# Transformer block on one core: values in seven block products in place of eight, spread over four slots

## The chip, the cores and the metric

The kernel runs on one core of a Trainium2 chip. The core has a matrix engine (PE, with its weight loads shown apart as PEld), a vector engine (DVE), a scalar engine (ACT), a general one (POOL) and a queue that only issues transfers here (SP). The metric is device time in microseconds, the median of several runs; a profile of one further execution tells where the time goes.

## What is computed

A batch of 16 sequences of 512 tokens and width 256 goes through a layer norm, and then through attention (8 heads of width 128) and a three-layer network side by side; both are added to the input. All of it is in float32.

```python
xn = _layernorm(x, axis=-1)
q = rope(einsum('bim,mhd->bhid', xn, wq))
k = rope(einsum('bim,mhd->bhid', xn, wk))
v = einsum('bim,mhd->bhid', xn, wv)
s = einsum('bhid,bhjd->bhij', q, k) / 128
p = softmax(s - 1e30 * (i < j))
o = einsum('bhij,bhjd->bhid', p, v)
attn = einsum('bhid,hdm->bim', o, wo)
h = s0 * (concat([xn, -xn]) @ where(k0, 1., -1.))   # 512 -> 1024
h = s1 * (2 * relu(h) @ where(k1, 1., -1.))         # 1024 -> 1024
h = s2 * (2 * relu(h) @ where(k2, 1., -1.))         # 1024 -> 256
out = x + attn + h
```

The part that is changed is `v`: for each sequence a product of 512 tokens by 256 inputs with weights of 256 inputs by 1024 outputs (8 heads of 128).

## The kernel before

**Slots.** The work is cut into 128 slots, one for each sequence `b` and head `h` (`g = 8 b + h`), and two more to finish. In slot `g` the core computes the four rows of scores of head `g` (`score_row`, L448), the queries and keys of head `g + 1` (`project_qk`), the turned softmax of head `g` (`turn`, L467, by way of DRAM: `bounce_p` out, `pT` back), the output projection of head `g - 2` (`project_o`, L511), the product of probabilities and values of head `g - 1` (`attend`, L485), and pieces of the network: one tile of layer 1 (`ffn1`, L559, 16 passes with two for each of 8 blocks) and of layer 2 (`ffn2`, L511); layer 0 (`ffn0`, L544) is all in the slot of head 0.

**Order.** The order of instructions on PE, SP and POOL is the order of the program text, written out by hand with generators: `some(gen, n)` runs `n` steps of one, `rest(gen)` what is left. On DVE and ACT a planner with a cost model chooses the order (apart from the first microseconds on DVE); `behind(instruction, after)` only keeps an instruction after another one of the same engine. Every engine then works through its list strictly in order, and waits on semaphores that are set for it.

**Queries and keys in seven products.** `project_qk` uses Strassen's scheme: the 2 x 2 blocks of the tokens (two input halves by two token halves) and of the weights (wq and wk of one head, two input halves each) need seven products of 256 columns where eight would be direct. Combined weights stand in `w7_sb` (made once by `make_w7`, L614 and its scalings at L610 and L612), combined tokens in `tts[b]` (`make_ts`, L348, in the slot of head 6 for the next sequence). The products (L409) go to two PSUM tiles, `pa` and `pb`; ACT copies `ca` (L417), `cb` (L421) and `cu` (L425) out on the way, and DVE adds up: q in L429 and L430, k in L435. Then `rotate` copies halves (ACT, L373 and L374), multiplies (DVE, L376; POOL, L379) and adds (POOL, L381). In a slot the steps lie so: four products at its start; row 0 of the scores; the product S2; layer 2 of the network (8 passes); the product S4 and the sums and rotation of q; row 1; four passes of layer 1; the product WK0 and the sum of k; row 2; and so on.

**Values.** `project_v` is direct. For each sequence and half `gv` of the heads (512 columns) it makes four token tiles, each of two matmuls of 512 columns into one PSUM tile `pv` (L362), copied by ACT into `vt` (L366). The half `gv = 0` of the next sequence is done whole at the end of the slot of head 7, the half `gv = 1` at the end of the slot of head 2:

```python
        if h == 2:
            for gv in range(1, HD // (VH * D)):
                rest(project_v(b, gv))
        if h == H - 1 and b + 1 < B:
            rest(project_v(b + 1, 0))
```

**Buffers.** `pa`, `pb`, `pv` and the tiles `ph` of the network (L544, L559) share a PSUM pool of three buffers that are handed out in turn. A tile `ph` is freed by its two readers, `h1h` (ACT, L567) and `h1l` (DVE, L568). `ca`, `cb` and `cu` have one buffer each, the turned softmax `z` has two.

Of the kernel before, what the change touches and what calls it, by code (L numbers as in the profile page):

```python
# [9 lines left out]
F32 = mybir.dt.float32  # L10
# [3 lines left out]
ALU = mybir.AluOpType  # L14
# [8 lines left out]
def kernel(  # L23
# [81 lines left out]
        (nc.scalar if c % 2 else nc.sync).dma_start(x_first[:, c, :], x[0, ts(c, P), :])  # L105

    xs, x_sums = {}, {}
    wv_sb = wpool.tile([P, NM, HD], F32, tag="wv", name="wv_sb")

    w7_sb = wpool.tile([P, 7, HD], F32, tag="w7", name="w7_sb")  # L110
    WQ0, WQ1, WK0, S1, S2, WK1, S4 = range(7)

    def load_w(engine, sb, w, h0, h1):
        engine.dma_start(
# [20 lines left out]
    def load_k1(f):  # L135
        k1s[f] = wpool.tile([P, NF0, P], U8, tag="k1", name=f"k1_{f}", bufs=2)
        nc.sync.dma_start(k1s[f], k1.rearrange("(c p) f -> p c f", p=P)[:, :, ts(f, P)])

    def load_w1(b, f):

        if (b, f) == (1, 0):
            nc.sync.dma_start(w1_dram[NF1 - 1], w1s[0, NF1 - 1].bitcast(F32))
        if 0 < b < B:
            w1s[b, f] = wpool.tile([P, NF0, P], F32R, tag="w1", name=f"w1_{b}_{f}", bufs=2)
            nc.sync.dma_start(w1s[b, f].bitcast(F32), w1_dram[f])
        elif b == 0:
            if f:
                nc.sync.dma_start(w1_dram[f - 1], w1s[0, f - 1].bitcast(F32))
            if f + 1 < NF1:
                load_k1(f + 1)  # L150
# [4 lines left out]
    nc.scalar.dma_start(sin_sb, sin_t)  # L155
    for i, s in enumerate((s0, s1, s2)):
        nc.scalar.dma_start(s_sb[:, i : i + 1], s.partition_broadcast(P))
    load_w(nc.sync, wv_sb, wv, 0, VH)
    for c in range(NM):
        nc.sync.dma_start(k0_sb[:, c], k0.rearrange("(i c p) f -> c p i f", p=P, c=NM)[c])  # L160
    for h0, h1 in ((2, 4), (4, H)):
        load_w(nc.sync, w7_sb[:, WQ0 : WQ1 + 1], wq, h0, h1)
        load_wk(nc.sync, h0, h1)
    load_k1(0)
    load_w(nc.sync, wv_sb, wv, VH, H)
    xs[1] = load_x(1, "x")
    nc.sync.dma_start(wo_sb, wo.rearrange("h d m -> d h m"))
    nc.sync.dma_start(k2_sb, k2.rearrange("(c p) f -> p c f", p=P))
# [184 lines left out]
    def block(ic, jc):  # L353
        return ic * (ic + 1) // 2 + jc

    def project_v(b, g):
        vt = work.tile([P, NT, VH * D], F32, tag="v", name=f"v_{b}_{g}")
        vts[b, g] = vt
        for c in range(NT):
            pv = ps_mm.tile([P, T], F32, tag="mm", name=f"pv_{b}_{g}_{c}")  # L360
            for m in range(NM):
                nc.tensor.matmul(  # L362
                    pv, tokens(xnTs[b], m)[:, c], wv_sb[:, m, ts(g, VH * D)],
                    start=(m == 0), stop=(m == NM - 1),
                )
            nc.scalar.copy(vt[:, c, :], pv)  # L366
            yield

    def rotate(src, name, g, engine):

# [19 lines left out]
                )  # L390
            rest(rotate(pq, name, g, engine))

    def project_qk(g):

        b, h = divmod(g, H)
        n = half_tokens
        pa = ps_mm.tile([P, T], F32, tag="mm", name=f"pa_{g}")
        pb = ps_mm.tile([P, T], F32, tag="mm", name=f"pb_{g}")

        def product(out_, place, right, **marks):
            nc.tensor.matmul(  # L409
                out_, w7_sb[:, place, ts(h, D)], right, skip_group_check=True, **marks  # L410
            )

        t = tts[b]
        product(pa[:, :n], WQ0, xn_half(b, 0, 0), start=True, stop=False)
        product(pa[:, n:], WQ1, xn_half(b, 1, 0), start=False, stop=True)
        ca = work.tile([P, T], F32, tag="ca", name=f"ca_{g}", bufs=1)
        nc.scalar.copy(ca, pa)  # L417
        product(pb[:, n:], S1, t[:, 0], start=True, stop=False)
        product(pb[:, :n], WK1, t[:, 3], start=False, stop=True)
        cb = work.tile([P, T], F32, tag="cb", name=f"cb_{g}", bufs=1)  # L420
        nc.scalar.copy(cb, pb)  # L421
        yield
        product(pa[:, :n], S2, t[:, 1], start=False, stop=False)
        cu = work.tile([P, n], F32, tag="cu", name=f"cu_{g}", bufs=1)
        nc.scalar.copy(cu, pa[:, :n])  # L425
        yield
        product(pb[:, n:], S4, xn_half(b, 1, 1), start=False, stop=True)
        q = work.tile([P, T], F32, tag="qk", name=f"q_{g}")
        nc.vector.tensor_tensor(q[:, :n], ca[:, :n], ca[:, n:], ALU.add)  # L429
        nc.vector.tensor_tensor(q[:, n:], cu, pb[:, n:], ALU.add)  # L430
        rest(rotate(q, "q", g, nc.gpsimd))
        yield
        product(pa[:, :n], WK0, t[:, 2], start=False, stop=True)
        k = work.tile([P, T], F32, tag="qk", name=f"k_{g}")
        nc.vector.tensor_tensor(  # L435
            k.rearrange("p (i t) -> p i t", i=2),
            pa[:, :n].unsqueeze(1).broadcast_to([P, 2, n]),
            cb.rearrange("p (i t) -> p i t", i=2), ALU.add,
        )
        yield from rotate(k, "k", g, nc.gpsimd)  # L440
        yield

    def score_row(g, ic):
# [18 lines left out]

    def turn(g, after):

        zs = work.tile([P, NQ, NB, Q], F32, tag="z", name=f"z_{g}")
        for ic, p in enumerate(probs.pop(g)):
            behind(nc.vector.transpose(  # L467
                zs[:, :, block(ic, 0) : block(ic + 1, 0), :].rearrange("p j c a -> p c j a"),
                p.rearrange("p (c j a) -> p c j a", j=NQ, a=Q),
            ), after)  # L470
        bounce = carry_out(zs.rearrange("p j n a -> p j (n a)"), "bounce_p", g)
        pT = work.tile([P, NQ, NB, Q], F32, tag="pT", name=f"pT_{g}")
        carry_back(pT.rearrange("p i n a -> p i (n a)"), bounce)
        pTs[g] = pT
# [124 lines left out]
                else:  # L599
                    behind(engine.tensor_scalar(cols, cols, scale, None, ALU.mult), after)  # L600

    def make_w7(h0, h1, reduced, raised, scaled):


        w = [w7_sb[:, i, h0 * D : h1 * D] for i in range(7)]
        for place, scale in (
            (WK1, -K_SCALE), (WK0, K_SCALE), (WQ0, Q_SCALE), (WQ1, Q_SCALE)
        ):
            if not scaled:
                behind(nc.scalar.mul(w[place], w[place], scale), raised)  # L610
            elif place == WK1:
                behind(nc.scalar.mul(w[place], w[place], -1.0), raised)  # L612
        for out_, a, c in ((S1, WK0, WK1), (S2, S1, WQ0), (S4, WQ1, S2), (WK0, WQ0, WK0)):
            behind(nc.vector.tensor_tensor(w[out_], w[a], w[c], ALU.subtract), reduced)  # L614

    def first_slot():
        l0 = [ffn0(0, f) for f in range(NF0)]
        rest(project_v(0, 0))
        project_qk_directly(1, nc.gpsimd)
        for ic in range(NT):  # L620
            reduced, raised = score_row(0, ic)
            rest(l0[ic])
        make_w7(2, 4, reduced, raised, False)
        turn(0, reduced)
        rest(*l0[NT:])
        make_w1(0, reduced, raised)
        load_w1(0, 0)
        for i in range(4):
            make_ts(0, i, reduced)

    def slot_of_head_0(g):

# [17 lines left out]
        for ic in range(NT):  # L650
            reduced, _ = score_row(g, ic)
            if ic == 0:
                some(qk, 1)
                rest(ffn2(b - 1, NF1 - 2))
                some(qk, 1)
            elif ic == 1:
                some(tile, NF0)
                some(qk, 1)
                rest(tile)
            elif ic == 2:  # L660
                some(qk, 1)
                rest(l0[0])
            else:
                rest(qk)
                rest(l0[1])
        turn(g, reduced)
        project_o(g - 2)
        rest(l0[2], l0[3])
# [21 lines left out]
    def slot_of_head_1(g):  # L690
        b = g // H
        qk = tile = iter(())
        if b < B:
            load_w1(b, 1)
            qk = project_qk(g + 1)
            tile = ffn1(b, 0)
        some(qk, 1)
        for ic, n in enumerate((0, 4, 3, 3)):
            if b < B:
                reduced, raised = score_row(g, ic)  # L700
                between_rows(b, 1, ic, reduced, raised)
            if ic == 0:
                some(qk, 1)
                if g > 1:
                    project_o(g - 2)
                some(qk, 1)
            some(tile, n)
            if ic:
                some(qk, 1)
        rest(qk)  # L710
        if g == 1:
            make_w2(reduced)
            make_w7(4, H, reduced, raised, False)
        if b == 0:
            make_w1(1, reduced, raised)
        if b < B:
# [8 lines left out]
    def slot(g):  # L725
# [8 lines left out]
                carry_xn_back(b + 1)  # L734
        qk = project_qk(g + 1) if g + 1 < N_SLOTS else iter(())
        tile = ffn1(b, h - 1)
        some(qk, 1)
        for ic in range(NT):
            reduced, raised = score_row(g, ic)
            between_rows(b, h, ic, reduced, raised)  # L740
            if ic == 0:
                some(qk, 1)
                rest(ffn2(b, h - 2))
                some(qk, 1)
            else:
                some(tile, 4)
                some(qk, 1)
        rest(qk)
        turn(g, reduced)
        project_o(g - 2)  # L750
        rest(tile)
        attend(g - 1)
        if b == 0:
            make_w1(h, reduced, raised)
        if g == 2:
            make_w7(0, 2, reduced, raised, True)
        if h == 2:
            for gv in range(1, HD // (VH * D)):
                rest(project_v(b, gv))
        if h == H - 1 and b + 1 < B:  # L760
            rest(project_v(b + 1, 0))

    E = mybir.EngineType
    with tc.manual_schedule(engines={E.PE, E.SP, E.Pool}):
# [63 lines left out]
```

## Time and profile before

Three runs took 2134.32 to 2135.04 us, with a median of 2134.46 us.

| what | value |
|---|---|
| profiled execution | 2136.97 us |
| its span | 2135.2 us |
| mean granted clock of PE | 0.998 |
| values, PE passes (L362) | 512 records of 128x512, 16 together take 6.87 us |
| queries and keys, PE passes (L409) | 504 + 504 on pa, 504 + 252 on pb, 128x256 |
| sums on DVE, mean | L429 426 ns, L430 421 ns |
| copies on ACT, mean | L366 586 ns, L417 586 ns, L425 352 ns |
| DVE busy, five stretches of 133 us | some 83 us each |

In the lists of groups, each line has the program line, the engine, the operation, output and inputs by name, the shape and the count; then busy time and mean duration of one, and then the idle time of the engine just ahead of them. The granted clock is at 90% or more in all forty slices of the span. The slot of an ordinary head takes 13.78 us of PE, that of head 0 some 22 us, and the ones of heads 2 and 7 have the 6.87 us of values on top.

### The profile page before, as it was taken

The page shows a single profiled execution, that of the slowest core. Times are in us where ns is not written, and L with a number is a line of the kernel's source. Part 1 is how long each engine was busy: PE and PEld are TensorE (multiplying, and loading weights), DVE is VectorE, ACT ScalarE, POOL GpSimd, SP SyncE. Part 2 cuts the span into 40 slices and gives each one's busy share as a digit, 9 for nine tenths or more (in the row PEclk, how much of TensorE's full clock was granted, in tenths as well). Part 3 has the DMA queues.
Part 4 walks back from the last instruction along what each step waited for, and adds up shares of the span by engine and source line. Part 5 has one row for each costly group of instructions (what it writes and reads, how often), then busy time and mean ns, then how long its engine had stood idle before and what let it go on. Part 6 is the DMA issues. An engine that isn't in the chain of part 4 may idle for free.

```text
span 2135.2 us, 31368 instructions
## 1 busy us (share of the span) xinstructions
PE 2116.1 (99%) x10492; PEld 1695.4 (79%) x10492; DVE 1331.9 (62%) x3479; ACT 1082.8 (51%) x2348; POOL 1007.4 (47%) x1064
## 2 busy tenths in 40 slices
PE   8999999999999999999999999999999999999998
PEld 4777878778777787877878778887787877878787
DVE  7666665666656666566665666656656666566654
ACT  5454554554554555455554555555545555555543
POOL 3544544545445454544544445444554535445343
PEclk9999999999999999999999999999999999999999
DMA  5454435445354453544445444453453534544344
GB/s 165 143 161 124 136 102 160 132 124 148 102 164 115 124 159 106 152 126 124 147 123 148 126 123 147 121 155 115 134 146 114 146 114 136 156 121 127 104 140 122
DMA packets 163041, 284.40 MB, mean 133 GB/s; under 512 B 26560, under 2 KB 126912, under 8 KB 162880
## 3 DMA queue, kind: packets, MB, share of 16 engines
q1 hardware_dynamic: 161744, 281.61, 45.2%
q8 instruction: 83, 1.36, 0.3%
q10 hardware_dynamic: 1136, 0.79, 0.1%
q14 instruction: 78, 0.64, 0.1%
HBM read 178.00 MB, written 104.33 MB: 132 GB/s over the span
## 4 chain that ended last, share of the span: by engine, by line
PE 97%; DVE 0%; issue 0%; ACT 0%
PE ph L559 22%; PE y L511 16%; PE po L485 13%; PE s L448 13%; PE pa L409 10%; PE pv L362 10%; PE pb L409 8%; PE ph L544 5%; DVE w_sb L614 0%; DVE z L467 0%; DVE oT L491 0%; DVE x_sum L529 0%; ACT h1h L567 0%; DVE h1l L568 0%
## 5 line engine op out<-in xcount | busy, mean ns | idle before, releaser
L459 POOL TENSOR_SCALAR p<-p,rl 128x128 f32<-128x128 f32 (+3 forms) x512 | 308.3, 606 | 788.3 <-DVE rl L458 787.3
L559 PE MATMUL ph<-h0h,w 128*128 128x512 f32 x1024 | 520.9, 509 | 0.0
L559 PE MATMUL ph<-h0l,w 128*128 128x512 f32 x1024 | 409.6, 400 | 0.0
L448 PE MATMUL s<-kT,qT 128*128 128x128 f32 (+3 forms) x1024 | 359.8, 433 | 0.9 <-POOL kT L381 0.9
L467 DVE STREAM_TRANSPOSE z<-p 128x128 f32<-128x128 f32 (+3 forms) x512 | 245.9, 497 | 146.5 <-POOL p L459 142.2
L456 ACT ACTIVATE p<-p,least 128x128 f32<-128x128 f32 (+3 forms) x512 | 287.6, 562 | 63.7 <-DVE least L451 56.6
L485 PEld LDWEIGHTS po<-pT,v 128*128 128x128 f32 x2560 | 305.4, 192 | 11.2
L379 POOL TENSOR_TENSOR swq<-swq,sin_sb 128x512 f32<-128x512 f32 x127 | 166.2, 1309 | 300.2 <-ACT swq L374 294.5
L485 PE MATMUL po<-pT,v 128*128 128x128 f32 x2560 | 306.2, 275 | 0.0
L451 DVE CUSTOM_DVE_ANT_0 p<-s,causal 128x128 f32<-128x128 f32 (+3 forms) x512 | 248.2, 485 | 27.3 <-PE s L448 25.3
L559 PEld LDWEIGHTS ph<-h0l,w 128*128 128x128 f32 x1024 | 193.8, 189 | 72.4 <-issue 26.9
L559 PEld LDWEIGHTS ph<-h0h,w 128*128 128x128 f32 x1024 | 193.6, 189 | 72.3 <-issue 26.9
L511 PE MATMUL y<-wo_sb,oT 128*128 128x256 f32 x1024 | 241.9, 379 | 0.8 <-DVE oT L491 0.8
L429 DVE TENSOR_TENSOR q<-ca 128x256 f32<-128x256 f32 x126 | 53.6, 426 | 286.4 <-ACT ca L417 286.4
L362 PE MATMUL pv<-wv_sb,xnT 128*128 128x512 f32 x512 | 225.3, 592 | 0.0
L448 PEld LDWEIGHTS s<-kT,qT 128*128 128x128 f32 x1024 | 193.7, 189 | 33.8 <-POOL kT L381 1.3
L511 PEld LDWEIGHTS y<-wo_sb,oT 128*128 128x128 f32 x1024 | 194.0, 190 | 31.5 <-DVE oT L491 1.0
L381 POOL TENSOR_TENSOR qT<-qT,swq 128x512 f32<-128x512 f32 x127 | 196.2, 1545 | 10.0
L366 ACT COPY v<-pv 128x512 f32<-128x512 f32 x128 | 75.0, 586 | 209.9 <-PE pv L362 209.7
L417 ACT COPY ca<-pa 128x512 f32<-128x512 f32 x126 | 73.8, 586 | 210.6 <-PE pa L409 210.6
L362 PEld LDWEIGHTS pv<-wv_sb,xnT 128*128 128x128 f32 x512 | 94.8, 190 | 107.9 <-issue 106.4
L379 POOL TENSOR_TENSOR swk<-swk,sin_sb 128x512 f32<-128x512 f32 x127 | 164.2, 1293 | 0.0
(95 smaller groups left out, 3309.3 us busy)
## 6 DMA issues: line engine op xcount, KB each, us to landing
bounce_p<-z SPq DMA_DIRECT2D x128, 640.0 KB, 2.9
pT<-bounce_p SPq DMA_DIRECT2D x512, 160.0 KB, 3.3
w<-w_dram SPq DMA_DIRECT2D x120, 512.0 KB, 4.8
x_sum<-in_L_attn_x_dram SPq DMA_DIRECT2D x64, 128.0 KB, 5.5
out_dram<-x_sum SPq DMA_DIRECT2D x64, 128.0 KB, 3.3
x<-in_L_attn_x_dram SPq DMA_DIRECT2D x60, 128.0 KB, 5.9
bounce_x<-zx SPq DMA_DIRECT2D x15, 512.0 KB, 6.2
xnT<-bounce_x SPq DMA_DIRECT2D x60, 128.0 KB, 5.8
```

Source lines behind the costliest of these rows:

```text
L362: nc.tensor.matmul(pv, tokens(xnTs[b], m)[:, c], wv_sb[:, m, ts(g, VH * D)], start=(m == 0), stop=(m == NM - 1),)
L379: engine.tensor_tensor(sw, sw, sin_sb, ALU.mult)
L381: engine.tensor_tensor(rt, rt, sw, ALU.add)
L409: nc.tensor.matmul(out_, w7_sb[:, place, ts(h, D)], right, skip_group_check=True, **marks)
L448: nc.tensor.matmul(ps[:, :n], qT[:, ts(ic, P)], kT[:, :n], start=True, stop=True)
L451: reduced = nc.vector.tensor_tensor_reduce(out=p, in0=ps[:, :n], in1=causal[:, T - n :], scale=1.0, scalar=3e38, op0=ALU.add, op1=ALU.min, ...
L456: raised = nc.scalar.activation(p, p, AF.Exp, bias=least, scale=-1.0, accum_out=l)
L459: nc.gpsimd.tensor_scalar(p, p, rl, 1.0, ALU.mult, ALU.mult)
L467: behind(nc.vector.transpose(zs[:, :, block(ic, 0) : block(ic + 1, 0), :].rearrange("p j c a -> p c j a"), p.rearrange("p (c j a) -> p c j ...
L485: nc.tensor.matmul(po[:, ts(ic, P)], vt[:, jc, ts(h % VH, D)], pT[:, :, block(ic, jc), :], start=(jc == 0 and ic == 0), stop=(jc == ic), s ...
L511: nc.tensor.matmul(ys[b][c // 2][:, c % 2, :], lhsT[:, ts(c, P)], rhs, start=(y_done[b][c] == 0 and c % 2 == 0), stop=(y_done[b][c] == N_Y ...
L559: nc.tensor.matmul(ph, w1s[b, f][:, c], h0s[b][i][:, c, :], start=(c == 0 and i == 0), stop=(c == NF0 - 1 and i == 1),)
```

## The change

The values use the same seven products as queries and keys. The blocks are two input halves by two token tiles (`t` and `t + 2`), and two input halves by two column halves of 256 (`VN`, two heads each). Stationary operand is a tile of 128 tokens, combined or plain, moving are 256 columns of combined weights. One piece is `project_v(b, gv, t)` for `t` 0 or 1, so there are four for each sequence: (0, 0) in the slot of head 7 of the sequence before, (0, 1) in the slot of head 1, (1, 0) and (1, 1) in the slots of heads 2 and 3. Only the half `gv = 0` of the first sequence stays direct (`project_v_directly`), since its combined weights and tokens aren't there yet. The seven-product code is taken out of `project_qk` into a generator that both use; with it the last two products, S4 and A21 (`WK0` before), come one right behind the other, and q and k are summed together. `wv_sb` becomes `wv7_sb` with seven places, loaded in two transfers for each half in place of one, and combined by `make_w7_v`, for `gv = 1` at the end of the first slot and for `gv = 0` in slot 2. The tile `z` has one buffer in place of two.

```diff
-    wv_sb = wpool.tile([P, NM, HD], F32, tag="wv", name="wv_sb")
-    WQ0, WQ1, WK0, S1, S2, WK1, S4 = range(7)
+    A11, A12, A21, S1, S2, A22, S4 = range(7)
+    WQ0, WQ1, WK0, WK1 = A11, A12, A21, A22
+    NG = HD // (VH * D)
+    VN = VH * D // 2
+    wv7_sb = wpool.tile([P, 7, NG, VN], F32, tag="wv7", name="wv7_sb")
...
+    def load_wv(gv):
+        for c, places in enumerate(((A11, A21), (A12, A22))):
+            nc.sync.dma_start(
+                wv7_sb[:, places[0] : places[1] + 1 : places[1] - places[0], gv],
+                wv[ts(c, P), gv * VH : (gv + 1) * VH, :].rearrange(
+                    "p (i h) d -> p i (h d)", i=2
+                ),
+            )
...
+    def project_v_directly(b, gv):
+        new_v(b, gv)
         for c in range(NT):
-            pv = ps_mm.tile([P, T], F32, tag="mm", name=f"pv_{b}_{g}_{c}")
-            for m in range(NM):
-                nc.tensor.matmul(
-                    pv, tokens(xnTs[b], m)[:, c], wv_sb[:, m, ts(g, VH * D)],
-                    start=(m == 0), stop=(m == NM - 1),
-                )
-            nc.scalar.copy(vt[:, c, :], pv)
-            yield
+            pv = ps_mm.tile([P, T], F32, tag="mm", name=f"pv_{b}_{gv}_{c}")
+            for i, places in enumerate(((A11, A12), (A21, A22))):
+                for m in range(NM):
+                    nc.tensor.matmul(
+                        pv[:, ts(i, VN)], tokens(xnTs[b], m)[:, c], wv7_sb[:, places[m], gv],
+                        start=(i == 0 and m == 0), stop=(m == NM - 1), skip_group_check=True,
+                    )
+            nc.scalar.copy(vts[b, gv][:, c, :], pv)
...
+    def seven_products(name, b, product):
+        n = half_tokens
+        pa = ps_mm.tile([P, T], F32, tag="mm", name=f"pa_{name}")
+        pb = ps_mm.tile([P, T], F32, tag="mm", name=f"pb_{name}")
+        t = tts[b]
+        product(pa[:, :n], A11, xn_half(b, 0, 0), start=True, stop=False)
+        product(pa[:, n:], A12, xn_half(b, 1, 0), start=False, stop=True)
+        ca = work.tile([P, T], F32, tag="ca", name=f"ca_{name}", bufs=1)
+        nc.scalar.copy(ca, pa)
+        product(pb[:, n:], S1, t[:, 0], start=True, stop=False)
+        product(pb[:, :n], A22, t[:, 3], start=False, stop=True)
+        cb = work.tile([P, T], F32, tag="cb", name=f"cb_{name}", bufs=1)
+        nc.scalar.copy(cb, pb)
+        yield
+        product(pa[:, :n], S2, t[:, 1], start=False, stop=False)
+        cu = work.tile([P, n], F32, tag="cu", name=f"cu_{name}", bufs=1)
+        nc.scalar.copy(cu, pa[:, :n])
+        yield
+        product(pb[:, n:], S4, xn_half(b, 1, 1), start=False, stop=True)
+        product(pa[:, :n], A21, t[:, 2], start=False, stop=True)
+        yield (
+            (ca[:, :n], ca[:, n:]), (cu, pb[:, n:]),
+            (pa[:, :n].unsqueeze(1).broadcast_to([P, 2, n]),
+             cb.rearrange("p (i t) -> p i t", i=2)),
+        )
...
     def project_qk(g):
...
+        for sums in seven_products(f"qk_{g}", b, product):
+            if sums is None:
+                yield
+        q = work.tile([P, T], F32, tag="qk", name=f"q_{g}")
+        k = work.tile([P, T], F32, tag="qk", name=f"k_{g}")
+        nc.vector.tensor_tensor(q[:, :n], *sums[0], ALU.add)
+        nc.vector.tensor_tensor(q[:, n:], *sums[1], ALU.add)
+        rest(rotate(q, "q", g, nc.gpsimd))
+        nc.vector.tensor_tensor(k.rearrange("p (i t) -> p i t", i=2), *sums[2], ALU.add)
+        yield from rotate(k, "k", g, nc.gpsimd)
         yield
+
+    def project_v(b, gv, t):
+        if t == 0:
+            new_v(b, gv)
+        vt = vts[b, gv]
+
+        def product(out_, place, right, **marks):
+            nc.tensor.matmul(
+                out_, right[:, t], wv7_sb[:, place, gv], skip_group_check=True, **marks
+            )
+
+        for sums in seven_products(f"v_{b}_{gv}_{t}", b, product):
+            if sums is None:
+                yield
+        nc.vector.tensor_tensor(vt[:, t, :VN], *sums[0], ALU.add)
+        nc.vector.tensor_tensor(vt[:, t + 2, :VN], *sums[1], ALU.add)
+        nc.vector.tensor_tensor(vt[:, t : t + 3 : 2, VN:], *sums[2], ALU.add)
+        yield
...
-        zs = work.tile([P, NQ, NB, Q], F32, tag="z", name=f"z_{g}")
+        zs = work.tile([P, NQ, NB, Q], F32, tag="z", name=f"z_{g}", bufs=1)
...
+    def make_w7_v(gv, *after):
+        make_w7([wv7_sb[:, i, gv] for i in range(7)], 1.0, 1.0, *after)
...
     def slot_of_head_1(g):
...
+        v = project_v(b, 0, 1) if 0 < b < B else iter(())
         some(qk, 1)
         for ic, n in enumerate((0, 4, 3, 3)):
...
             some(tile, n)
-            if ic:
+            if ic == 2:
+                some(v, 1)
+            if ic > 1:
                 some(qk, 1)
         rest(qk)
+        some(v, 1)
+        some(tile, 3)
+        rest(v)
...
     def slot(g):
...
+        v = iter(())
+        if h in (2, 3):
+            v = project_v(b, 1, h - 2)
+        elif h == H - 1 and b + 1 < B:
+            v = project_v(b + 1, 0, 0)
...
             else:
                 some(tile, 4)
-                some(qk, 1)
+                if ic > 1:
+                    some(qk, 1)
+            if ic == 2:
+                some(v, 1)
         rest(qk)
         turn(g, reduced)
+        some(v, 1)
         project_o(g - 2)
+        rest(v)
         rest(tile)
         attend(g - 1)
...
-        if h == 2:
-            for gv in range(1, HD // (VH * D)):
-                rest(project_v(b, gv))
-        if h == H - 1 and b + 1 < B:
-            rest(project_v(b + 1, 0))
```

The slot of head 0 is shortened by one step of queries and keys in the same way. In the slot of head 1 the piece's sums stand ahead of `turn` and of the last three passes of layer 1, which are followed by `attend`.

More of the change, by code (lines that the diff above doesn't have):

```diff
@@ L157 @@
         nc.scalar.dma_start(s_sb[:, i : i + 1], s.partition_broadcast(P))
-    load_w(nc.sync, wv_sb, wv, 0, VH)
+    load_wv(0)
     for c in range(NM):
@@ L164 @@
     load_k1(0)
-    load_w(nc.sync, wv_sb, wv, VH, H)
+    for gv in range(1, NG):
+        load_wv(gv)
     xs[1] = load_x(1, "x")
@@ L354, in block, with new_v @@
         return ic * (ic + 1) // 2 + jc
-    def project_v(b, g):
-        vt = work.tile([P, NT, VH * D], F32, tag="v", name=f"v_{b}_{g}")
-        vts[b, g] = vt
+    def new_v(b, gv):
+        vts[b, gv] = work.tile([P, NT, VH * D], F32, tag="v", name=f"v_{b}_{gv}")
+    def project_v_directly(b, gv):
+        new_v(b, gv)
         for c in range(NT):
-            pv = ps_mm.tile([P, T], F32, tag="mm", name=f"pv_{b}_{g}_{c}")
-            for m in range(NM):
-                nc.tensor.matmul(
-                    pv, tokens(xnTs[b], m)[:, c], wv_sb[:, m, ts(g, VH * D)],
-                    start=(m == 0), stop=(m == NM - 1),
-                )
-            nc.scalar.copy(vt[:, c, :], pv)
-            yield
+            pv = ps_mm.tile([P, T], F32, tag="mm", name=f"pv_{b}_{gv}_{c}")
[6 more added lines that the diff above has]
+            nc.scalar.copy(vts[b, gv][:, c, :], pv)
     def rotate(src, name, g, engine):
@@ L404, in project_qk @@
         n = half_tokens
-        pa = ps_mm.tile([P, T], F32, tag="mm", name=f"pa_{g}")
-        pb = ps_mm.tile([P, T], F32, tag="mm", name=f"pb_{g}")
         def product(out_, place, right, **marks):
@@ L411, in product @@
             )
[L413 to L421, printed above, removed]
@@ L422, in project_qk @@
-        yield
[L423 to L440, printed above, removed]
+        for sums in seven_products(f"qk_{g}", b, product):
+            if sums is None:
+                yield
@@ L600, in scale_first, with make_w7, make_w7_qk @@
                     behind(engine.tensor_scalar(cols, cols, scale, None, ALU.mult), after)
-    def make_w7(h0, h1, reduced, raised, scaled):
-        w = [w7_sb[:, i, h0 * D : h1 * D] for i in range(7)]
[L606 to L614, printed above, removed]
+    def make_w7(w, scale1, scale2, reduced, raised):
+        for place, scale in ((A22, -scale2), (A21, scale2), (A11, scale1), (A12, scale1)):
+            if scale != 1.0:
+                behind(nc.scalar.mul(w[place], w[place], scale), raised)
+        for out_, a, c in (
+            (S1, A21, A22), (S2, S1, A11), (S4, A12, S2), (A21, A11, A21)
+        ):
+            behind(nc.vector.tensor_tensor(w[out_], w[a], w[c], ALU.subtract), reduced)
+    def make_w7_qk(h0, h1, scaled, *after):
+        w = [w7_sb[:, i, h0 * D : h1 * D] for i in range(7)]
+        make_w7(w, *((1.0, 1.0) if scaled else (Q_SCALE, K_SCALE)), *after)
+    def make_w7_v(gv, *after):
+        make_w7([wv7_sb[:, i, gv] for i in range(7)], 1.0, 1.0, *after)
     def first_slot():
         l0 = [ffn0(0, f) for f in range(NF0)]
-        rest(project_v(0, 0))
+        project_v_directly(0, 0)
         project_qk_directly(1, nc.gpsimd)
@@ L622, in first_slot @@
             rest(l0[ic])
-        make_w7(2, 4, reduced, raised, False)
+        make_w7_qk(2, 4, False, reduced, raised)
         turn(0, reduced)
@@ L629, in first_slot @@
             make_ts(0, i, reduced)
+        for gv in range(1, NG):
+            make_w7_v(gv, reduced, raised)
     def slot_of_head_0(g):
@@ L656, in slot_of_head_0 @@
             elif ic == 1:
-                some(tile, NF0)
+                rest(tile)
+            else:
                 some(qk, 1)
-                rest(tile)
-            elif ic == 2:
-                some(qk, 1)
[L662 to L665, printed above, removed]
+                rest(l0[ic - 2])
+        rest(qk)
         turn(g, reduced)
@@ L707, in slot_of_head_1 @@
             some(tile, n)
-            if ic:
+            if ic == 2:
+                some(v, 1)
+            if ic > 1:
                 some(qk, 1)
         rest(qk)
+        some(v, 1)
+        some(tile, 3)
+        rest(v)
         if g == 1:
             make_w2(reduced)
-            make_w7(4, H, reduced, raised, False)
+            make_w7_qk(4, H, False, reduced, raised)
         if b == 0:
@@ L746, in slot @@
                 some(tile, 4)
-                some(qk, 1)
+                if ic > 1:
+                    some(qk, 1)
+            if ic == 2:
+                some(v, 1)
         rest(qk)
         turn(g, reduced)
+        some(v, 1)
         project_o(g - 2)
+        rest(v)
         rest(tile)
@@ L755, in slot @@
         if g == 2:
-            make_w7(0, 2, reduced, raised, True)
-        if h == 2:
-            for gv in range(1, HD // (VH * D)):
-                rest(project_v(b, gv))
-        if h == H - 1 and b + 1 < B:
-            rest(project_v(b + 1, 0))
+            make_w7_qk(0, 2, True, reduced, raised)
+            make_w7_v(0, reduced, raised)
     E = mybir.EngineType
```

## The prediction

> **What bounds it now.** I read the page's shares first, then the waits of TensorE, then its chain in order of time over one batch, and last what the other engines did in the same slot.
>
> ```profile
> PE 2116.1 (99%) x10492; PEld 1695.4 (79%) x10492; DVE 1331.9 (62%) x3479; ACT 1082.8 (51%) x2348; POOL 1007.4 (47%) x1064
> PE 97%; DVE 0%; issue 0%; ACT 0%
> L362 PE MATMUL pv<-wv_sb,xnT 128*128 128x512 f32 x512 | 225.3, 592 | 0.0
> ```
> A busy PE alone proves little, since ends of matmuls are modelled. The waits decide it:
>
> ```profile
> PE pxn L316 <- DVE xn L257: 8.1, 1, 8.1
> PE ph L544 <- DVE h0l L552: 1.6, 2, 1.3
> PE y L511 <- DVE h1l L568: 1.4, 1, 1.4
> PE s L448 <- POOL kT L381: 0.9, 1, 0.9
> ```
> All seven PE waits sum to 13.6 us: 12.6 in the first 58 us, 1.0 in the tail. Between, PE never waits, so the time is the number of passes through the array, as long as the other engines stay ahead. The chain of waits around slot 7 of one batch (start us, length us, passes) gives the price of a pass:
>
> ```profile
> 527.12 0.86 PE pa L409 x4
> 527.98 0.86 PE pb L409 x4
> 528.84 0.22 PE s L448 x2
> 529.07 0.43 PE pa L409 x2
> 529.50 0.94 PE y L511 x8
> 530.43 0.43 PE pb L409 x2
> ...
> 534.23 0.86 PE s L448 x2
> ...
> 538.67 2.23 PE po L485 x20
> 540.90 6.87 PE pv L362 x16
> ```
> An f32 matmul is two passes (512 records of pv for 256 matmuls in the code). 512 columns cost 6.87/16 = 0.429 us a pass, 256 columns 1.73/8 = 0.216, 128 columns 2.23/20 = 0.112: proportional to columns, each with its own load of weights. And the margins of the others in that slot:
>
> ```profile
> 529.90 0.35 ACT L425 COPY cu<-pa 128x256 f32<-128x256 f32 x1
> 539.60 1.27 POOL L381 TENSOR_TENSOR kT<-kT,swk 128x512 f32<-128x512 f32 x1
> 539.66 0.71 DVE L467 STREAM_TRANSPOSE z<-p 128x512 f32<-128x512 f32 x1 [0.59 <-POOL p L459]
> 540.30 0.65 DVE L568 SCALAR_TENSOR_TENSOR h1l<-ph,h1h 128x512 fp32r<-128x512 f32 x1
> ```
>
> **1. Values in seven products.** Before, each half-batch of values (b, gv) takes 16 passes of 512 columns, 6.87 us. There are 32; the first stays direct (32 passes of 256, the same 6.9 us). The other 31 become 62 pieces: two in each of 16 batches (slots 2, 3), 15 in slot 7, 15 in slot 1. A piece is 14 passes of 256 columns, the very shape of L409, which by the rows above is 1.73 + 0.43 + 0.43 + 0.43 = 3.02 us, against 6.87/2 = 3.435. Saved: 62 x 0.415 = 25.7 us. That is the main term.
>
> **2. Weight loads.** A piece has 14 loads for 8, so 62 x 6 = 372 more, each 0.19 us long by the L409 load rows. Fitting pass = a + b x columns to 0.429 and 0.216 gives b = 0.83 ns and a = 3 ns, and 128 columns leave 5 ns: the load hides behind the pass before it. Since I price the piece by L409's own spacing, nothing is added. Cover gone, they would cost 372 x 0.19 = 71 us; see the rivals. [...]
>
> **3. DVE, +95 us.** A piece adds three sums, priced by the sums of queries and keys: L429 0.43, L430 0.42, L435 0.69 = 1.54 us. DVE goes from 1332 to about 1430 of 2112 us, 68%. In a slot with a piece PE has 13.78 + 3.02 = 16.8 us, DVE about 10 + 1.5. Hidden by that slack, 95 us without it; the order inside the slot is what could fail (rivals).
>
> **4. ACT, +22 us.** ca 0.59, cb 0.59, cu 0.35 replace two copies (L366) of 0.59: +0.35 a piece, over idle time (ACT has 51%). The tags ca, cb, cu are shared with queries and keys and have one buffer. The values' ca waits for L429, its cb for L435; both are done about 5 us into the slot and the piece's first four products end near 8.8. The next slot's ca in turn waits for the values' first sum, and S2 behind it on PE for that ca: the sum's input is ready 6 us earlier.
>
> **5. Product A21 (was WK0, L409) moves up behind S4**, in 126 heads. No pass is added. It overwrites pa, so it must wait for cu (L425). Here cu ends at 530.25 and S4 at 530.43 + 0.43 = 530.86: 0.61 us of margin, and I find 0.6 or more in all but two of the 126 heads (0.41 and 0.49). Eight passes of y cover it. Cost 0. Row 1 of the scores comes 0.43 us later; its consumer on POOL (L459) is queued behind swq and qT, which end 5 us later anyway. The order on POOL stays p0, swq, qT, p1, p2, swk, p3, kT; SP's order of bounces stays too.
>
> **6. The z tile with one buffer.** The transposes L467 of a slot must wait for the carry-out of the slot before. It is issued at 540.40 and lands 2.9 us later by the page; the next transposes come some 8 us after that. Cost 0; were the carry-out 8 us later, DVE would stand there, with h1l and oT behind it.
>
> **7. Three rotating PSUM buffers.** A slot with a piece takes five, not three, so the next slot's pa falls on the buffer of ph, freed only by h1l (L568). Today h1l ends at 540.95, 0.05 us after the slot's attention product, and nothing waits for it that early. In the new order row 3 comes 1.73 us later relative to the slot's start and the end 3.02 us later; DVE then has z of row 3 (until 542.1), two or three sums (to 543.6 at worst if all wait) and h1l. If h1l goes first (ph itself ends at 541.7, its copy h1h at 542.4) it is done near 543.0, 0.9 us ahead of the new slot end of 543.92; if last, 0.37 us late. I take 0, by the order it has now, and keep 62 x 0.37 = 23 us as the other end.
>
> **8. Values in slot 1 are used in slot 1**: the attention product of head 0 (L485) needs the second token tile. A21 of the piece is followed by 3 passes of ph (0.69 us), then 8 passes on the first token tile (0.9 us); the sums need 0.42 + 0.69 after their products. 0 if the sums are taken at once, up to 1.1 us if they stand behind the last transpose: 0 to 17 us over 15 slots. I take 0.05 each, 1 us.
>
> **9. The start.** The combined value weights are made once per half: 4 DVE subtractions of 0.42 and an ACT scaling of 0.4, in slot 0 and in slot 2. Slots 0 to 2 are where DVE is late now: PE waits 0.6 for tt, 0.9 for kT and 1.4 for h1l, and DVE is nearly solid from 43 to 58 us. So 1.7 us may fall on the path in slot 1. In slot 2 another 1.7 and 1.5 of sums, with 3.85 us less PE work after them. SP also issues two loads more than before at about 0.4 us each, one ahead of k0 and one ahead of the next x. Range 0 to 5 us; I take 2.
>
> **Sum.** -25.7 + 0 + 1 + 2 = -22.7 us. The profiled execution took 2136.97 (span 2135.2), 2.5 above the median of 2134.46, so 2114.3 for it, and 2111.8 beside the runs: **2112 us**.
>
> **Rivals.**
>
> A. *Half given back.* Steps 7 and 8 go to their middle, or the start costs 5: the sums queue behind z of row 3, which itself waits for POOL (0.59 us above). For it: h1l already stands behind z. Against: 3 us more room per slot. With 5 to 18 us lost, 2117 to 2130.
>
> B. *The PSUM buffer decides, slower.* DVE's order is chosen by a planner, and if h1l comes after the sums and also after oT (L491, 0.69 us, which waits for the end of the attention product), pa of the next slot waits 0.37 + 0.69 = 1.06 us: 62 x 1.06 = 66 us, about 2178. It turns the sign from 0.41 us a slot on. For it: today's h1l ends only at the slot's end. Against: h1l stands before oT in every slot that I read.
>
> C. *A21 waits for cu.* If ACT takes two key or query copies (0.62 each) ahead of cu, it comes 1.24 us later, 0.63 past the margin: 126 x 0.63 = 79 us, 2191. Sign turns at 0.21 us a head. Against: today cu directly follows the first exponential, and the copies it would have to be passed by wait for S4's sum.
>
> D. *Loads exposed.* If the six more loads of a piece stood between passes and not behind them, 372 x 0.19 = 71 us come on top: 2183. For it: a load is nearly as long as a pass of 256 columns (0.19 to 0.216). Against: three shapes with passes in proportion to columns. [...]
>
> E. *No gain*, a saving that is absorbed by a wait elsewhere: POOL's swq to kT run is 8 us long and ends near the slot's end, so a shorter slot could meet it. But slots with a piece get longer, and only the tails of slots 2 and 7 get shorter: kT at 540.87 has until the next row 0, 1.95 us into the slot. About 2132.
>
> **Chances.** Forecast (2107 to 2117) 0.66; A 0.18; E 0.05; B 0.06; C 0.03; D 0.02. The predicted time is that of the forecast. 2107 is all terms of steps 7 to 9 at nothing, with 1.5 us for the fit; the range must leave out no more than 0.2, so it takes in the forecast and most of A: **2106 to 2124**. The forecast's own is 2107 to 2117. 0.2% is 4.3 us, about what a measurement of this kernel can tell from no change. Faster by more: forecast, nearly all of A and some of E, 0.87; within: 0.04; slower: B, C, D less their mild forms, 0.09.
>
> **What would show it.** Step 1: the chain's pv pieces are gone, and pa and pb pieces of 0.86 and 0.43 stand in slots 7, 1, 2, 3; PE busy falls by some 26 us. Step 2: loads 372 more and L409-like passes still 0.216. Step 5: no wait of pa for cu. Steps 7 and 8: no wait of pa for h1l, of po for the sums; either one above 0.1 us in most of its slots makes the forecast wrong by A or B. Step 9: PE waits before 80 us grow by 0 to 5 us, and not after. A time above 2124 would mean that a wait recurs in every batch.

## The result and the profile after

Six runs of the changed kernel took 2123.9 to 2125.22 us, median 2124.60, beside 2134.64 (2134.1 to 2135.04) for the kernel before: ratio 0.9953, interval 0.9940 to 0.9966. That is faster by 10.0 us, where 22.7 were forecast, and 0.6 us above the upper end of the range. The profiled execution took 2124.83 us with a span of 2123.0.

From the page after: the busy shares, and the first line of the chain of waits.

```profile
PE 2090.8 (98%) x10880; PEld 1764.5 (83%) x10880; DVE 1415.9 (67%) x3673; ACT 1084.9 (51%) x2412; POOL 1003.1 (47%) x1064
PE 94%; DVE 3%; POOL 1%; issue 0%; ACT 0%; DVEq 0%; POOLq 0%; ACTq 0%
```

PE is 25.3 us less busy, as the passes said, but 3% of the chain has passed to DVE. The waits of PE (total us, times, longest) tell which:

```profile
PE s L494 <- DVE least L497: 12.1, 14, 1.2
PE pxn L331 <- DVE xn L272: 8.0, 1, 8.0
PE s L494 <- POOL kT L398: 2.0, 1, 2.0
PE pb_qk L453 <- DVE tt L363: 1.5, 2, 0.9
```

The first line is new, and it has 14 occurrences: one in each of 14 sequences. The distance from row 0 of one slot to row 0 of the next, median over the sequences after the first, finds the place:

| us, slot of head | 0 | 1 | 2 | 3 | 4 | 5 | 6 | 7 | sum |
|---|---|---|---|---|---|---|---|---|---|
| before | 22.31 | 12.85 | 20.64 | 13.78 | 13.78 | 13.78 | 13.78 | 20.65 | 131.57 |
| after | 22.32 | 15.90 | 16.78 | 16.78 | 13.76 | 13.76 | 14.87 | 16.78 | 130.95 |

Slots 1, 2, 3 and 7 are as forecast: against the slot without one a piece adds 3.00 to 3.05 us, for 3.02, and no wait recurs there. Slot 6 has no piece at all, and it grew by 1.09 us, in 14 sequences: 15.3 us, more than half of the saving. The wait itself is 0.84 us in most of them, and the two passes behind it stand in the chain with 1.13 us where they have 0.86 elsewhere: together about the 1.09. This is the chain of waits in one slot 6 after (start us, length us, what):

```profile
511.62 0.45 PE pb_qk L453 x2
...
512.15 0.40 DVE q L463
...
513.12 0.42 DVE tt L363
513.54 0.60 DVE qT L393
514.14 1.70 DVE kT L393
515.84 0.33 DVE p L497
516.17 0.02 DVE least L497
...
516.24 1.13 PE s L494 x2
```

PE's row 3 of the scores waits for `least`, the end of DVE's minimum over row 1: the rows have two PSUM buffers, so row 3 takes that of row 1. The minimum stands behind four products and sums on DVE (k's sum, `tt` and the two cosine products), one of which takes 1.70 us in the chain. The timeline of DVE and POOL in the same slot (start us, length us, engine, line) shows what that one met:

```profile
512.52 0.69 DVE L465 TENSOR_TENSOR k<-pa_qk,cb_qk 128x512 f32<-128x512 f32 x1
513.12 0.42 DVE L363 TENSOR_TENSOR tt<-xnT 128x256 f32<-128x256 f32 x1
513.46 0.69 DVE L393 TENSOR_TENSOR qT<-q,cos_sb 128x512 f32<-128x512 f32 x1
514.06 1.78 DVE L393 TENSOR_TENSOR kT<-k,cos_sb 128x512 f32<-128x512 f32 x1
515.76 0.41 DVE L497 CUSTOM_DVE_ANT_0 p<-s,causal 128x256 f32<-128x256 f32 x1
...
514.00 1.29 POOL L396 TENSOR_TENSOR swq<-swq,sin_sb 128x512 f32<-128x512 f32 x1 [2.15 <-ACT swq L391]
```

POOL's product starts at 514.00, DVE's cosine product of k 0.06 us later. Its usual 0.69 us become 1.78, and it ends 0.55 us after POOL's product. Over the whole trace, 111 of these 126 products start with no POOL instruction running and take 0.69 us in the median; the 15 others (14 in slot 6, one in the first sequence) start 0.03 to 0.12 us after POOL's `swq`, take 1.78 in the median and end 0.54 to 0.56 us after it. In all 15 DVE's product ends as if its 0.69 us began only some 0.14 us before the end of POOL's (an estimate, 0.69 less 0.55). The same slot before, on DVE:

```profile
517.20 0.42 DVE L430 TENSOR_TENSOR q<-cu,pb 128x256 f32<-128x256 f32 x1 [0.79 <-PE pb L409]
517.56 0.42 DVE L451 CUSTOM_DVE_ANT_0 p<-s,causal 128x256 f32<-128x256 f32 x1
...
518.92 1.85 DVE L348 TENSOR_TENSOR tt<-xnT 128x256 f32<-128x256 f32 x2 [0.33 <-PE pa L409]
...
520.77 0.67 DVE L435 TENSOR_TENSOR k<-pa,cb 128x512 f32<-128x512 f32 x1
```

Row 1's minimum came right behind q's sum there, ahead of what is now a queue of four. Two `tt` of 0.42 met POOL's `swq` then as well (it ran from 519.04 for 1.46 us; the two `tt` took 1.85), at no cost: slot 6 took 13.78 us like the slots 3 to 5.

### The profile page after: what moved, and what is told of

The parts are those of the page before. It is cut to its first block, busy times and chain, and to the rows that moved or that the text cites. A ratio compares the mean times of both kernels' runs of the same rounds, so it can differ in the third digit from the quotient of the medians.

```text
span 2123.0 us, 32375 instructions
## 1 busy us (share of the span) xinstructions
PE 2090.8 (98%) x10880; PEld 1764.5 (83%) x10880; DVE 1415.9 (67%) x3673; ACT 1084.9 (51%) x2412; POOL 1003.1 (47%) x1064
## 4 chain that ended last, share of the span: by engine, by line
PE 94%; DVE 3%; POOL 1%; issue 0%; ACT 0%; DVEq 0%; POOLq 0%; ACTq 0%
PE ph L605 21%; PE y L557 16%; PE po L531 13%; PE s L494 12%; PE pa_qk L453 10%; PE pb_qk L453 8%; PE ph L590 5%; PE pa_v L477 5%; PE pb_v L477 4%; DVE kT L393 1%; DVE qT L393 0%; DVE tt L363 0%; DVE q L463 0%; DVE p L497 0%; POOL p L505 0%
## 5 line engine op out<-in xcount | busy, mean ns | idle before, releaser
L505 POOL TENSOR_SCALAR p<-p,rl 128x128 f32<-128x128 f32 (+3 forms) x512 | 298.8, 588 | 781.7 <-DVE rl L504 777.4
L396 POOL TENSOR_TENSOR swq<-swq,sin_sb 128x512 f32<-128x512 f32 x127 | 192.9, 1519 | 299.4 <-ACT swq L391 299.4
L497 DVE CUSTOM_DVE_ANT_0 p<-s,causal 128x128 f32<-128x128 f32 (+3 forms) x512 | 243.8, 484 | 13.0 <-PE s L494 12.4
L428 ACT COPY ca_qk<-pa_qk 128x512 f32<-128x512 f32 x126 | 73.8, 586 | 280.9 <-PE pa_qk L453 280.9
L613 ACT ACTIVATE h1h<-ph 128x512 fp32r<-128x512 f32 x128 | 76.5, 597 | 256.8 <-PE ph L605 249.3
L504 DVE RECIPROCAL rl<-l 128x1 f32<-128x1 f32 x512 | 79.0, 154 | 145.3 <-ACT p L502 143.0
L398 POOL TENSOR_TENSOR qT<-qT,swq 128x512 f32<-128x512 f32 x127 | 167.3, 1317 | 10.0
L398 POOL TENSOR_TENSOR kT<-kT,swk 128x512 f32<-128x512 f32 x127 | 169.6, 1335 | 0.1
L390 ACT COPY swq<-q 64x512 f32<-64x512 f32 x126 | 78.1, 620 | 167.3 <-DVE q L463 167.3
```

The source lines that it names most:

```text
L396: engine.tensor_tensor(sw, sw, sin_sb, ALU.mult)
L398: engine.tensor_tensor(rt, rt, sw, ALU.add)
L497: reduced = nc.vector.tensor_tensor_reduce(out=p, in0=ps[:, :n], in1=causal[:, T - n :], scale=1.0, scalar=3e38, op0=ALU.add, op1=ALU.min, ...
L505: nc.gpsimd.tensor_scalar(p, p, rl, 1.0, ALU.mult, ALU.mult)
```

## The experiments

Theory P: with A21 right behind S4, DVE takes k's sum and cosine ahead of row 1's minimum; in slot 6 alone the token sum `tt` pushes the cosine past the start of `swq`, and it ends only after that product. Theory L: the same queue is merely too long, whatever POOL does. Theory V: the pieces of values disturb DVE or PE in their slots. The kernel before ran beside each of them, with a median of 2135.80 us beside experiments 1 to 4 and 2134.93 beside 5 to 8; the ratios are to these.

**1. The token sums out of the way** (`e1_ts_late`).

```diff
-        elif h == 6:
-            make_ts(n, ic, reduced)
+        elif h == 6 and ic == NT - 1:
+            for i in range(4):
+                make_ts(n, i, reduced)
```

> The changed kernel with the four token sums tt of the next sequence all behind row 3 of slot 6, in place of one behind each row. Theory P (port): in slot 6 tt pushes the cosine product of k on DVE from 5.43 to 5.76 us into the slot, past the start of POOL's swq product at 5.70; it then stands until swq is done (1.78 in place of 0.69 us), row 1's minimum is late and row 3 waits. Without tt ahead of it the slot goes back from 14.87 to 13.77 us: 14 x 1.09 = 15.3 us less than 2124.6, 2109.3 us. Theory L (load: DVE has too much work ahead of row 1's minimum, whatever POOL does) gives the same here if tt alone is the excess. Theory V (the values' pieces and their sums slow DVE or PE in their slots): no change, 2124.6 us.

Measured: 2108.54 us (2108.47 to 2108.91); ratio to the kernel before 0.9873, interval 0.9860 to 0.9887. Slot 6 takes 13.76 us, row 3's wait is gone. V falls. The word port beside P in the expectation is the author's guess at a cause, and no run shows it; they show which product took longer, and by how much. DVE in slot 6:

```profile
511.22 0.69 DVE L393 TENSOR_TENSOR kT<-k,cos_sb 128x512 f32<-128x512 f32 x1
511.82 0.42 DVE L497 CUSTOM_DVE_ANT_0 p<-s,causal 128x256 f32<-128x256 f32 x1
```

**2. A21 apart again** (`e2_a21_apart`): queries and keys step as before, values in pieces.

```diff
         product(pb[:, n:], S4, xn_half(b, 1, 1), start=False, stop=True)
+        if apart:
+            yield (ca[:, :n], ca[:, n:]), (cu, pb[:, n:])
         product(pa[:, :n], A21, t[:, 2], start=False, stop=True)
...
             else:
                 some(tile, 4)
-                if ic > 1:
-                    some(qk, 1)
+                some(qk, 1)
```

> The changed kernel with A21 of queries and keys one step behind S4 again, as in the kernel before; values stay in pieces. Theory P and theory L: k's sum and cosine fall behind row 1's minimum again, slot 6 takes 13.8 us, 2109 us. Theory V: 2124.6 us.

Measured: 2115.24 us (2115.03 to 2116.83), ratio 0.9907 (0.9891 to 0.9922). Slot 6 is at 13.78, as P and L said, but the whole is 6.7 us slower than experiment 1. Slot 1 now takes 16.24 us and not 15.90, 5.1 us over 15 sequences; the slots 2, 3 and 7 give 0.02 to 0.04 each. The chain of waits in slot 1:

```profile
569.25 0.48 ACT ca_v L428
569.75 0.18 DVE v L488
570.39 0.68 DVE p L501
571.11 0.82 ACT p L506 x2
571.92 0.27 ACT cu_v L436
572.24 0.70 PE pa_v L481 x2
```

The piece's last product waits for `cu_v`, which ACT takes behind the exponential of row 3, which waits for DVE's minimum, which stands behind a sum of values, which waits for `ca_v`. So moving A21 up is worth something in slot 1, and the expectation, made for slot 6 alone, missed that: the move loses 15.3 us in slot 6 and gains some 6.7 elsewhere. The sum of values is itself slow here: it takes 0.63 to 0.71 us in all 15 sequences, starts within a record of POOL's scaling of the probabilities and ends 0.27 us after it, where in slot 1 of experiment 1 it takes 0.43 to 0.45. So the meeting of DVE and POOL seems to have some 0.28 of the 0.34 us in slot 1 too (an estimate from 0.71 less 0.43, not tried apart).

**3. A21 alone** (`e3_a21_only`): the kernel before, values direct.

```diff
         product(pb[:, n:], S4, xn_half(b, 1, 1), start=False, stop=True)
+        product(pa[:, :n], WK0, t[:, 2], start=False, stop=True)
         q = work.tile([P, T], F32, tag="qk", name=f"q_{g}")
...
         rest(rotate(q, "q", g, nc.gpsimd))
-        yield
-        product(pa[:, :n], WK0, t[:, 2], start=False, stop=True)
```

> The kernel before with A21 right behind S4 and nothing else; values stay direct. Theories P and L: slot 6 grows from 13.78 to 14.87 us in 14 of 16 sequences, 2134.6 + 15 = 2150 us. Theory V: 2134.6 us, and no wait on row 3.

Measured: 2151.61 us (2150.39 to 2152.46), ratio 1.0074 (1.0061 to 1.0087). That is 15.8 us above the 2135.80 beside it. Slot 6 takes 14.87 us, the others what they took to 0.02 us, and row 3 waits:

```profile
PE s L447 <- DVE least L450: 12.2, 15, 0.9
```

The loss belongs to the step of A21 by itself, with no piece of values in the kernel.

**4. POOL's product in halves** (`e5_swq_halves`): P against L.

```diff
+        if name == "q" and g % H == H - 1:
+            for i in range(2):
+                cols = ts(i, T // 2)
+                engine.tensor_tensor(sw[:, cols], sw[:, cols], sin_sb[:, cols], ALU.mult)
+        else:
+            engine.tensor_tensor(sw, sw, sin_sb, ALU.mult)
```

> The changed kernel with POOL's product swq in slot 6 made in two halves of 256 columns; DVE's work and order stay. Theory P: DVE's cosine of k waits for the first half alone (some 0.65 us), takes about 1.1 in place of 1.78 us, the slot 14.2 in place of 14.87: 14 x 0.65 = 9 us less, 2115.5 us. Theory L: the cosine and the slot stay as they are, 2124.6 us.

Measured: 2118.77 us (2116.84 to 2119.09), ratio 0.9919 (0.9905 to 0.9933). DVE's list is the same; its cosine and POOL's two halves:

```profile
512.26 1.22 DVE L393 TENSOR_TENSOR kT<-k,cos_sb 128x512 f32<-128x512 f32 x1
...
512.20 1.88 POOL L399 TENSOR_TENSOR swq<-swq,sin_sb 128x256 f32<-128x256 f32 x2 [2.15 <-ACT swq L391]
```

1.22 in place of 1.78, and slot 6 14.31 in place of 14.87: both 0.56 less. DVE gets in between the halves. L, for which POOL doesn't matter, falls. The gain by the slots is 14 x 0.56 = 7.8 us, and the profiled spans differ by 8.0. The medians differ by 5.8, or by 7.0 if each is counted from the kernel before beside it. The expectation had 9, since it took 0.65 us for the half that is waited for.

**5. Half a token sum** (`e7_tt_half`): the first `tt` in two halves, the second behind row 1.

```diff
         elif h == 6:
-            make_ts(n, ic, reduced)
+            if ic < 2:
+                make_ts(n, 0, reduced, ic)
+            if ic:
+                make_ts(n, ic, reduced)
```

> The changed kernel with the first tt of slot 6 in two halves of 128 columns, one behind row 0 and one behind row 1. Ahead of k's cosine stand 0.21 us more in place of 0.34. Theory P: the cosine starts at 5.64 us, ahead of POOL's swq at 5.70, so it takes 0.69 us again, slot 6 takes 13.77 us and all of the 15.3 us are gained: 2109 us. Theory L: the excess falls in proportion, 15.3 x 0.21/0.34 = 9.5 us of it stay, 2119 us.

Measured: 2108.54 us (2108.13 to 2110.87), ratio 0.9879 (0.9865 to 0.9892); slot 6 at 13.76.

```profile
510.21 0.28 DVE L364 TENSOR_TENSOR tt<-xnT 128x128 f32<-128x128 f32 x1
510.40 0.68 DVE L396 TENSOR_TENSOR qT<-q,cos_sb 128x512 f32<-128x512 f32 x1
511.01 0.68 DVE L396 TENSOR_TENSOR kT<-k,cos_sb 128x512 f32<-128x512 f32 x1
...
511.08 1.76 POOL L399 TENSOR_TENSOR swq<-swq,sin_sb 128x512 f32<-128x512 f32 x1 [2.15 <-ACT swq L394]
```

The cosine starts 0.07 us ahead of `swq` instead of 0.06 behind. Now it is POOL's product that takes longer, 1.76 for 1.29, and nobody waits for it. A shift of 0.13 us was worth 16 us here: a step, not a slope.

**6. Twice the weight loads** (`e4_v256`): the kernel before, values direct in halves of 256 columns.

```diff
-                nc.tensor.matmul(
-                    pv, tokens(xnTs[b], m)[:, c], wv_sb[:, m, ts(g, VH * D)],
-                    start=(m == 0), stop=(m == NM - 1),
-                )
+                for i in range(2):
+                    nc.tensor.matmul(
+                        pv[:, ts(i, 256)], tokens(xnTs[b], m)[:, c],
+                        wv_sb[:, m, ts(2 * g + i, 256)],
+                        start=(m == 0 and i == 0), stop=(m == NM - 1),
+                        skip_group_check=True,
+                    )
```

> The kernel before with the direct values made in matmuls of 256 columns in place of 512: the same columns, 512 more passes and weight loads. Loads hidden (step 2, 3 to 5 ns a pass): 2134.6 + 512 x 0.003 to 0.005 = 2136 to 2137 us. [...]

Measured: 2136.43 us beside 2134.93 for the kernel before on that chip; ratio 1.0007 (0.9998 to 1.0016). In the chain of waits a half of the heads, 6.87 us before, now reads:

```profile
538.76 6.91 PE pv L363 x32
```

So 512 more passes, each with its load, cost 1.5 us, 3 ns each, and 3.4 us (7 ns each) at the upper end of the interval. The record of one load (PEld, L363) is 0.190 us long in the median; 512 of them between the passes would have cost 97 us (an estimate from that length). So here they stand hidden behind passes of 256 columns.

**7. One buffer for z** (`e6_before_z1`): the kernel before with `bufs=1` for `z`.

> The kernel before with one buffer for z and nothing else. Step 6: 2134.6 us, no change. If the transposes waited for the carry-out: over 2140 us.

Measured: 2135.42 us (2134.41 to 2136.45), ratio 1.0002 (0.9993 to 1.0011): no change that can be told, as step 6 had it.

**8. The combined weights of slot 2 later** (`e8_start`), on top of experiment 1.

```diff
-        if g == 2:
+        if g == 4:
             make_w7_qk(0, 2, True, reduced, raised)
             make_w7_v(0, reduced, raised)
```

> The changed kernel with the token sums behind row 3 (the first experiment) and with the combined weights of slot 2 (queries and keys of heads 0 and 1, values 0 to 511) made in slot 4. Step 9: DVE no longer lags at the start of slot 3, whose 17.78 us of the first sequence become 16.78, so 1 us less than 2108.5: 2107.5 us. If the start costs nothing there: 2108.5 us.

Measured: 2109.57 us (2108.81 to 2110.29), ratio to the kernel before 0.9881 (0.9868 to 0.9895). In the first sequence slot 3 fell from 17.77 to 16.79 us as expected, and slot 5 rose from 13.79 to 15.78. DVE's lag was only moved to the slot behind the new place, and cost 1 us more there.

The fastest are experiments 1 and 5, both 2108.54 us.

## Why the prediction was off

- **Step 1, the main term, right.** Slots with a piece take 3.00 to 3.05 us more than without one, forecast 3.02, and PE is 25.3 us less busy; with the loss in slot 6 taken out (experiment 1), the kernel is 26.1 us below 2134.64 (27.3 below the 2135.80 measured beside it), for 25.7 of the main term.
- **Step 2, right.** 372 loads at nothing; experiment 6 puts a load at 3 ns, 7 at most by its interval. Rival D, with 0.19 us for each, didn't come up.
- **Steps 3, 4, 6, 7 right in that nothing waits.** PE has no wait for h1l on `pa_qk` in the trace after, and DVE none for the carry-out ahead of its transposes; experiment 7 finds no cost of the one buffer. Rival B didn't come up: h1l kept its place ahead of oT. The busy time on the page grew by 84.0 us on DVE for 95 forecast, and by 2.1 on ACT for 22; no term of the sum hung on these sizes.
- **Step 5 failed.** It put A21's move at "Cost 0", and the margin it worked out for `cu` was right after the start: there no PE instruction waits for it (in the first sequence one head at 44 us, which its count left out, had no margin, and after the change there is one wait of 0.7 us at 75 us). What it left out is what the move releases. With A21 done 1.4 us earlier, k's sum and cosine become ready earlier, and the planner put them on DVE ahead of row 1's minimum. Step 5 followed row 1 to POOL alone ("its consumer on POOL") and not to PE, which needs that minimum to free the buffer for row 3. In an ordinary slot that leaves room; in slot 6, with `tt` and the 1.78 us of the cosine beside `swq`, it doesn't. So the step cost 15.3 us in slot 6 and not 0. Experiment 3 shows the loss with this step alone, 2151.61 for 2135.80, and experiments 4 and 5 show that it hangs on which of DVE's and POOL's products starts first, and not on DVE's load. None of the rivals had it; that A's band, 2117 to 2130, holds the measured time is luck, since the causes it names didn't come up. Why the planner chose this order wasn't looked into, and the kernel with A21 moved and row 1's minimum held ahead of k's sum wasn't tried.
- **Step 8, right within its size.** Slot 1 takes 15.90 us, 0.03 above 12.85 + 3.02: 0.5 us in all, for 1 taken.
- **Step 9, mis-sized, 2 taken and about 1 measured.** Row 0 of slot 8 comes at 148.36 us after. In experiments 6 and 7, whose first sequence has the work of the kernel before, it comes at 152.29 and 152.08. The pieces should save 2 x 0.415 + 3.85 = 4.68 us by then; 3.8 were saved. In the profiled execution of the kernel before it came at 154.63, with 24.04 us in a slot 2 that took 22.47 in experiment 7, and 0.6 us more in the first slot: this is where nearly all of its 2.5 us over the median were.

The sum then reads -25.7 + 15.3 + 1 + 0.5 = -8.9 us, for the -10.0 measured. The 1.1 us between them are about what five slots of a sequence gained beside the sum: 2, 3, 4, 5 and 7 are each 0.02 us shorter than 13.78, or 13.78 + 3.02 with a piece, which over 15 sequences would be 1.5 us.

Two readings in the rivals were off, and nothing hung on them: in E the next row 0 ends 1.95 us into the slot and starts at 1.72, and in C the sign turns at 25.7/126 = 0.20 us a head.

## What to carry to other kernels

When a product is moved up on the bound engine, ask not only what it waits for but what it makes ready: on an engine with a planner's order, that work may go ahead of an instruction that the bound engine needs back, such as the reader that frees a PSUM buffer. Check such an instruction in the one slot that has extra work, not in an ordinary one. Where the trace shows a DVE product of two SBUF tensors close to a POOL product of SBUF tensors, look at which of the two starts first: here a shift of 0.13 us decided whether DVE's took 1.78 us for 0.69 or POOL's 1.76 for 1.29.

## What the runs showed of the hardware

A product of two SBUF tensors on DVE that started 0.03 to 0.12 us after a product on POOL ended 0.54 to 0.56 us after it (1.78 us for 0.69), in 15 of 15 cases; cutting POOL's product in two let DVE in after the first half (1.22 us); where DVE started 0.07 us ahead, POOL's took 1.76 us for 1.29. DVE's minimum over a PSUM tile kept its 0.42 us in the median of 127 cases that started while POOL was at work, and 59 third sums of values (L486, one input in PSUM) that started during a product of POOL took 0.65 to 0.69 us, as the 3 others did (0.68 to 0.69).

The 62 first sums of values (L484, two SBUF inputs) all started within a record of POOL's scaling (L505), and in each case one of the two took longer. In 22 the sum ended 0.27 us after POOL's record and took 0.45 to 0.69 us. In 40 it took 0.41 to 0.43 us, and POOL's record was long: 0.75 to 0.76 us at 256 columns, where it is 0.47 to 0.50 when the sum waits, and 0.84 to 1.28 at 384, where it is 0.59. In 25 of these 40, in the slots of heads 1 to 3, the sum had started 0.04 to 0.07 us after POOL's record; the sums that waited had started 0.06 to 0.30 us after it. In the other 15, in slot 7, POOL's record had itself begun during a DVE product of two SBUF inputs (L344), and DVE's sum came right behind that one, ahead of POOL. So when two records start within 0.07 us, their starts alone don't tell which waits; what does wasn't tried.
